# Two state space loops: every fourth product moves from VectorE to GpSimd, and the step sums from GpSimd to TensorE

## The chip, the cores and the metric

The kernel runs on one NeuronCore of one Trainium2 chip. Its engines work side by side, each on its own queue: TensorE (PE in the profile, its weight loads PEld), VectorE (DVE), ScalarE (ACT), GpSimd (POOL), and SyncE (SP), which here issues the DMA transfers. They wait for each other through semaphores. The metric is the time of one launch on the device in microseconds; lower is better.

## The reference, cut to what matters

A network of four layers with sixteen sub-blocks, all in float32, on x of 4 x 512 x 128. Two sub-blocks, L2b and L3b, are state space blocks (Mamba style), and only these are touched:

```python
x_dbl = u @ x_proj_w                     # u: 256 channels, from a convolution
dtr, Bc, Cc = x_dbl[..., :64], x_dbl[..., 64:80], x_dbl[..., 80:]
delta = softplus(dtr @ dt_proj_w + dt_proj_b)
A = -exp(A_log)                          # 256 channels x 16 states
def step(h, inp):
    d_t, b_t, c_t, u_t = inp
    dA = exp(d_t[:, :, None] * A)
    h = dA * h + (d_t * u_t)[:, :, None] * b_t[:, None, :]
    return h, einsum('bdn,bn->bd', h, c_t)
y = (ys + u * D) * silu(z)
out = y @ out_proj_w
```

For each of 4 batch rows there are 256 x 16 recurrences over 512 steps. Per recurrence: a decay (exp of step times A), a gain (step times u, times B), the scan, and a product with C that is summed over the 16 states.

## The kernel before, in words

The method `mamba` runs one such block. Its work is cut into units: a unit is 128 partitions x 2 x 512 steps, sixteen units make a batch row, 64 make the block. Two sub-blocks call it, so there are 128 units. The loop `for n in range(16 * B + 10)` issues, for each n, pieces of work for several units at once:

- `fetch(n + 5)`: SP copies the steps (`dl`, written to a DRAM tile before) back into one of six `da` tiles, spread over the partitions.
- `product(n + 1)` (line 2371): VectorE multiplies the gain by B (`br`), in place in PSUM.
- `scan(n)` (line 2376): VectorE's `tensor_tensor_scan` reads `da` from SBUF and the gain from PSUM and writes `hc` in SBUF. Line 2381: GpSimd multiplies `hc` by C (`cr`), in place. (For the last unit VectorE does it, line 2379.)
- `gain(n + 2)`: TensorE spreads `du` over the partitions, two matmuls into one of three `ps_du` buffers of two banks.
- `decay(n + 3)` (line 2357): ScalarE makes exp(A x step) in `da`, two activations.
- `read(m)`: every second n TensorE sums `hc` of two units, five and four behind, into `ps_y`.

Between these stand the pieces of `prepare(b)`, which makes the next batch row's inputs while the present one's units run: convolution halves (`c0a` to `c1b`), `u`, the projections `xd`, `br`, `cr`, the steps before softplus (`dt0`, `dt1`), `exps` and `logs` on ScalarE, the gates `z0`, `z1`, `sz`. Softplus is max(v,0) + ln(1 + exp(-|v|)), with a correction for the rounding of 1 + e. The sums that this takes (`s00` to `s13`, line 2274) are GpSimd operations of 128x512: three a half for the steps, and a fourth for `du` = steps x u. After the third the half is written to DRAM (line 2278).

The order on each engine is written out by hand: `keep` holds an instruction in program order on its engine, and the lists `order`, `usual` and `first` give each piece the n after whose unit work it is issued (`first` for batch row 1, whose preparation runs beside row 0's units; `usual` for rows 2 and 3). An engine's queue is in order, so a piece that waits holds back what is issued behind it.

PSUM is full: six banks for `ps_du`, one for `ps_y`, and one (tag "mm", the function `bank`) that all the preparing matmuls share in turn, each result being copied out by ScalarE before the next can begin.

I call the units 0 to 15 of a block group 0, and so on to group 3. In groups 0, 1 and 2 the next row is prepared; in group 3 nothing is.

Of the kernel before, what the change touches and what calls it, by code (L numbers as in the profile page):

```python
# [11 lines left out]
F32 = mybir.dt.float32  # L12
AF = mybir.ActivationFunctionType
ALU = mybir.AluOpType
# [4 lines left out]
P = 128  # L19
B, S, D = 4, 512, 128  # L20
# [254 lines left out]
class Net:  # L275
# [1895 lines left out]
    def mamba(self, g):  # L2171
# [5 lines left out]
        nc, tc = self.nc, self.tc  # L2177
        LAG, SPREAD, AHEAD, FETCH = 4, 2, 3, 5
        with ExitStack() as es:
            sp = es.enter_context(tc.tile_pool(name=g + "_s", bufs=1))  # L2180
            rp = es.enter_context(tc.tile_pool(name=g + "_r", bufs=2))
            pp = es.enter_context(tc.tile_pool(name=g + "_p", bufs=1, space=PSUM))
            dp = es.enter_context(tc.tile_pool(name=g + "_d", bufs=2, space=DRAM))
            keep = tc.keep_in_program_order
            m0 = self.m
            w, am, wc, dram = m0["w"], m0["am"], m0["wc"], m0["dram"]
            spread, gather, skip, ones = (m0[n] for n in ("spread", "gather", "skip", "ones"))
# [5 lines left out]
            def bank(name):  # L2193
                return pp.tile([P, S], F32, tag="mm", name=name)
# [3 lines left out]
            def prepare(b, **when):  # L2198

                u, sz, dl, du, br, cr = sets[b % 2]  # L2200
                xb = b * S
                t = {}
# [5 lines left out]
                def act(*a, **k):  # L2208
                    keep(nc.scalar.activation(*a, **k))
# [33 lines left out]
                    keep(nc.scalar.copy(out, ps[:n]))  # L2243

                def xd():
                    t["xd"] = rp.tile([64, S], F32, name="xd", bufs=1)
                    project(t["xd"], 0, 64)

                def step(c):
# [12 lines left out]

                def logs():
                    act(ln, w1, AF.Ln)
                    act(w1, w1, AF.Identity, bias=ones[:, 1:2])

                def sums(c, k):
                    o, x, y, op = (
                        (w1, w1, t["e"], ALU.subtract),
                        (ln, ln, w1, ALU.subtract),  # L2270
                        (dl, dl, ln, ALU.add),
                        (du, dl, u, ALU.mult),
                    )[k]
                    keep(nc.gpsimd.tensor_tensor(o[:, c], x[:, c], y[:, c], op))
                    if k == 2:
                        if c == 0:
                            dram[b] = dp.tile([P, 2, S], F32, name="dram")
                        nc.sync.dma_start(dram[b][:, c], dl[:, c])

                for name, n in when.items():  # L2280
                    f = {
                        "c0a": (conv, 0, False),
                        "c0b": (conv, 0, True),
                        "c1a": (conv, 1, False),
                        "c1b": (conv, 1, True),
                        "u": (lambda: act(u, t["raw"], AF.Silu),),
                        "xd": (xd,),
                        "dt0": (step, 0),
                        "dt1": (step, 1),
                        "br": (project, br, 64, P),  # L2290
                        "cr": (project, cr, 192, P),
                        "exps": (exps,),
                        "logs": (logs,),
                        "z0": (gate, 0),
                        "z1": (gate, 1),
                        "sz": (lambda: act(sz, t["z"], AF.Silu),),
                        **{f"s{c}{k}": (sums, c, k) for c in range(2) for k in range(4)},
                    }[name]
                    pieces.append((n, f))


            order = (
                "c0a", "c0b", "c1a", "c1b", "u", "xd", "dt0", "dt1", "br", "exps", "logs", "s00",
                "s01", "z0", "s02", "s10", "z1", "s11", "cr", "s12", "s03", "sz", "s13",
            )
            usual = (
                -6, -5, -4, -3, -2, -1, 0, 1, 2, 3, 4, 5,
                6, 6, 7, 8, 8, 9, 9, 10, 11, 11, 12,
            )
            for b in range(2, B):  # L2310
                at = {p: 16 * (b - 1) + n for p, n in zip(order, usual)}
                if b < B - 1:
                    at["sz"] += 3.5
                prepare(b, **at)
            first = (
                0, 0, 2, 2, 3, 4, 5, 6, 7, 7, 8, 8,
                9, 9, 9, 10, 9.5, 10, 8, 11, 11, 14.5, 12,
            )
            prepare(1, **dict(zip(order, first)))
            for n, f, *a in self.late:  # L2320
                pieces.append((n, (f, *a, bank)))
# [3 lines left out]
            dx, hc, yp, y, po = {}, {}, {}, {}, {}  # L2325
# [36 lines left out]
            def gain(n):  # L2362
                b, c, i, h = place(n)
                dx[n] = pp.tile([P, 2, S], F32, tag="du", name="ps_du", bufs=3)
                for t in range(2):
                    r = slice(64 * t, 64 * t + 64)
                    self.mm(dx[n][:, t], spread[r, 4 * h + i], sets[b % 2][3][r, c], pin=True)

            def product(n):
                br = sets[n // 16 % 2][4].unsqueeze(1).to_broadcast([P, 2, S])  # L2370
                keep(nc.vector.tensor_tensor(dx[n], dx[n], br, ALU.mult))  # L2371

            def scan(n):
                hc[n] = rp.tile([P, 2, S], F32, name="hc", bufs=7)
                h, a, x = (t.rearrange("p t s -> p (t s)") for t in (hc[n], da[n], dx[n]))
                keep(nc.vector.tensor_tensor_scan(h, a, x, 0.0, ALU.mult, ALU.add))  # L2376
                cr = sets[n // 16 % 2][5].unsqueeze(1).to_broadcast([P, 2, S])
                if n == 16 * B - 1:
                    keep(nc.vector.tensor_tensor(hc[n], hc[n], cr, ALU.mult))
                else:  # L2380
                    keep(nc.gpsimd.tensor_tensor(hc[n], hc[n], cr, ALU.mult))  # L2381
# [51 lines left out]
            for n in range(16 * B + 10):  # L2433
                if n + FETCH < 16 * B:
                    fetch(n + FETCH)
                if n + 1 < 16 * B:
                    product(n + 1)
                if n < 16 * B:
                    scan(n)
                if n + 2 < 16 * B:  # L2440
                    gain(n + 2)
                if n + AHEAD < 16 * B:
                    decay(n + AHEAD)
                while pieces and pieces[0][0] < n + 1:
                    f, *a = pieces.pop(0)[1]
                    f(*a)
                m = n - 1 - LAG
                if n % 2 == 1 and 0 <= m < 16 * B:
                    read(m)
                    if m % 8 == 6:  # L2450
                        last = m == 16 * B - 2
                        plan.at(n if last else n + 1, gated, m // 16, m // 8 % 2)
                        if m % 16 == 14:
                            plan.at(n if last else n + 4, output, m // 16)
                            plan.at(
                                n if last else n + 5,
                                lambda b: self.add_to_x(b, po[b], keep),
                                m // 16,
                            )
                plan.run(n)  # L2460
# [473 lines left out]
```

## Time and profile before

| what | value |
|---|---|
| runs shown | 2402.07 us median of 3 (2400.7 to 2405.41) |
| profiled execution | 2390.77 us, its span 2389.1 us |
| busy in the span | PE 2134.9, DVE 1703.8, ACT 1275.2, POOL 609.9 us |
| loop of L2b, first to last scan | 1577 to 1807 us |
| loop of L3b, first to last scan | 2110 to 2345 us |
| DMA in the loops | about 150 to 160 GB/s, half of the engines' time |

A line of the list of groups reads: source line, engine, operation, output<-inputs by name, shapes, count | busy us in all, mean ns of one | idle time of that engine just before, and who ended it. A line of a timeline reads: start, duration, engine, line, operation, and in brackets the idle time before it and its releaser. A float32 matmul appears as two MATMUL records. Matmuls overlap in their ends, so the distance from start to start tells more than a duration. The line number of a matmul is that of the helper, 346, so matmuls are told apart by their output's name.

### The profile page before, as it was taken

To read this page: it belongs to the slowest core of one execution; us is meant where nothing else is said; L and a number is where in the kernel's file an instruction comes from. 1 tells how busy PE (TensorE), PEld (TensorE's weight loads), DVE (VectorE), ACT (ScalarE), POOL (GpSimd) and SP (SyncE) were. 2 spreads that over 40 slices of the span, in tenths; PEclk is the share of its full clock that TensorE was granted. 3 is DMA by queue.
4 is the path that set the end of the run, shared out by engine and by line. 5 is a ranking of instruction groups with operands and counts; after the bars stand their busy time and mean duration, and the time that the engine had idled before them with its cause. 6 is when DMAs were issued, how large, how long until landed. Compare 5 with 4: busy or idle time off the path is not lost. (4 is left out here: it accounts for less than half of the span.)

```text
span 2389.1 us, 33451 instructions
## 1 busy us (share of the span) xinstructions
PE 2134.9 (89%) x12151; PEld 1004.9 (42%) x12151; DVE 1703.8 (71%) x3209; ACT 1275.2 (53%) x2539; POOL 609.9 (26%) x441
## 2 busy tenths in 40 slices
PE   7999999999899998999876889988969998878868
PEld 2343334643233333667434446542214666422213
DVE  6666666479998775556465664678997657688995
ACT  4555555169856655343442454666644445476643
POOL 1100010010000001022153410038872015148871
PEclk9999999999799998999876989999989999998989
DMA  3000000500000000600200016344552620044550
GB/s 145 1 1 1 1 1 19 126 1 1 2 2 2 1 2 1 144 1 2 109 0 1 1 32 102 71 120 144 156 154 43 113 41 2 1 132 138 158 154 18
DMA packets 68884, 127.84 MB, mean 54 GB/s; under 512 B 9328, under 2 KB 29296, under 8 KB 68080
## 3 DMA queue, kind: packets, MB, share of 16 engines
q1 hardware_dynamic: 68720, 125.71, 20.5%
q8 instruction: 96, 1.57, 0.3%
q14 instruction: 68, 0.56, 0.1%
HBM read 119.91 MB, written 5.64 MB: 53 GB/s over the span
## 5 line engine op out<-in xcount | busy, mean ns | idle before, releaser
L2381 POOL TENSOR_TENSOR hc<-hc,cr 128x1024 f32<-128x1024 f32 x126 | 297.2, 2359 | 113.9 <-DVE hc L2376 108.2
L2376 DVE TENSOR_TENSOR_SCAN hc<-da,ps_du 128x1024 f32<-128x1024 f32 x128 | 291.2, 2277 | 0.0
L346 PE MATMUL ps_s<-k,q 32*128 32x512 f32 (+3 forms) x1088 | 252.3, 601 | 8.6 <-DVE mx L853 4.7
L540 ACT ACTIVATE e<-ps_s,mx 128x512 f32<-128x512 f32 x256 | 172.6, 686 | 139.4 <-DVE mx L535 132.8
L346 PE MATMUL ps_du<-du,spread 64*128 64x512 f32 x512 | 161.6, 704 | 64.2 <-DVE hc L2376 63.9
L2357 ACT ACTIVATE da<-da,am 128x512 f32<-128x512 f32 x248 | 165.6, 715 | 62.5 <-DMA da<-dram 55.6
L346 PE MATMUL ps<-xT,w_L2f 128*128 128x512 f32 (+1 forms) x416 | 190.6, 605 | 0.2 <-DVE t L1948 0.2
L939 DVE TENSOR_REDUCE nm<-ps_s 128x1 f32<-128x512 f32 x256 | 162.5, 684 | 36.5 <-PE ps_s L346 24.2
L1025 ACT ACTIVATE e<-ps_st 128x512 f32<-128x512 f32 x256 | 138.3, 595 | 89.3 <-PE ps_s L346 61.5
L535 DVE TENSOR_REDUCE mx<-ps_s 128x2 f32<-128x1024 f32 x128 | 151.0, 1219 | 43.8 <-PE ps_s L346 43.6
L2371 DVE TENSOR_TENSOR ps_du<-ps_du,br 128x1024 f32<-128x1024 f32 x128 | 155.1, 1212 | 26.4 <-PE ps_du L346 26.4
L864 ACT ACTIVATE e<-e,mx 128x512 f32<-128x512 f32 (+3 forms) x256 | 140.1, 549 | 15.8 <-DVE mx L853 15.5
L346 PE MATMUL ps_st<-q,k 32*128 32x512 f32 x512 | 143.9, 646 | 0.0
L346 PE MATMUL ps_s<-q,k 64*128 64x512 f32 x512 | 129.1, 618 | 2.2 <-ACT e L540 1.7
L346 PE MATMUL ps_c<-e,vz 128*64 128x512 f32 x512 | 123.5, 604 | 0.8 <-POOL vz L551 0.8
L1948 DVE SCALAR_TENSOR_TENSOR t<-ps,w_L2f,t 128x512 f32<-128x512 f32 (+1 forms) x104 | 77.3, 747 | 61.8 <-PE ps L346 37.9
L661 DVE TENSOR_TENSOR hc<-hc,wt 128x1024 f32<-128x1024 f32 x80 | 93.6, 1171 | 36.5 <-DMA wt<-dram 17.5
L346 PEld LDWEIGHTS ps_du<-du,spread 64*128 64x128 f32 x512 | 45.3, 201 | 171.8 <-issue 126.4
L853 DVE CUSTOM_DVE_ANT_0 e<-ps_s,tri 128x512 f32<-128x512 f32 (+3 forms) x256 | 109.1, 484 | 11.7 <-PE ps_s L346 11.6
L346 PEld LDWEIGHTS ps_s<-k,q 32*128 32x128 f32 x1088 | 87.1, 194 | 71.8 <-issue 28.5
L551 POOL TENSOR_TENSOR vz<-v,z 128x512 f32<-128x512 f32 x32 | 33.3, 1042 | 322.0 <-DVE z L549 293.0
L346 PEld LDWEIGHTS ps<-xT,w_L2f 128*128 128x128 f32 (+1 forms) x416 | 74.8, 188 | 95.7 <-issue 78.7
(501 smaller groups left out, 4127.9 us busy)
## 6 DMA issues: line engine op xcount, KB each, us to landing
da<-dram SPq DMA_DIRECT2D x124, 256.0 KB
da<-dram SPq DMA_DIRECT2D x124, 255.5 KB
wt<-dram SPq DMA_DIRECT2D x144, 128.0 KB
wt<-dram SPq DMA_DIRECT2D x32, 256.0 KB
dram<-dl SPq DMA_DIRECT2D x16, 256.0 KB
wt<-dram SPq DMA_DIRECT2D x16, 224.0 KB
wt<-dram SPq DMA_DIRECT2D x16, 192.0 KB
wt<-dram SPq DMA_DIRECT2D x16, 160.0 KB
```

What stands on the lines that cost most here:

```text
L346: i = self.nc.tensor.matmul(out, lhsT, rhs, start=start, stop=stop)
L535: nc.vector.tensor_reduce(mx, sc, AX.X, ALU.max, negate=True)
L540: nc.scalar.activation(es[n][:, hh], sc[:, hh], AF.Exp, bias=mx[:, hh : hh + 1], accum_out=z[m][:, j, hh : hh + 1],)
L661: nc.vector.tensor_tensor(h, h, wt[b, k][:, r:e], ALU.mult)
L853: red = nc.vector.tensor_tensor_reduce(e[:, i, :w], sc[i][:, :w], tri[:, S - w :], -1.0, BIG, ALU.add, ALU.min, mx[:, i : i + 1],)
L864: nc.scalar.activation(e[:, i, :w], e[:, i, :w], AF.Exp, bias=mx[:, i : i + 1], scale=-1.0, accum_out=z[:, i : i + 1],)
L939: nc.vector.tensor_reduce(nm[:, j, i, 9:10], sc, AX.X, ALU.max, negate=True)
L1025: keep(nc.scalar.activation(es_[n][:, i], sc, AF.Exp))
L2357: nc.scalar.activation(da[n][:, t, t:], src[:, t:], AF.Exp, scale=am[:, at : at + 1])
L2371: keep(nc.vector.tensor_tensor(dx[n], dx[n], br, ALU.mult))
L2376: keep(nc.vector.tensor_tensor_scan(h, a, x, 0.0, ALU.mult, ALU.add))
L2381: keep(nc.gpsimd.tensor_tensor(hc[n], hc[n], cr, ALU.mult))
```

## The change

Three things, all in `mamba`:

1. For every fourth unit (n % 4 == 2, "shared") `product` is no longer a VectorE operation in PSUM. ScalarE copies the gain from PSUM to the unit's `hc` tile, GpSimd multiplies it there by B, the scan reads `da` and this `hc` (both in SBUF) and writes over it, and GpSimd then multiplies by C as before. `gain(n + 2)` and the shared product are issued before `scan(n)`. There are eight `hc` buffers in place of seven.
2. The three GpSimd sums of the steps go. `logs` now makes 1 - (1 + e) with the sign turned, and `total(c)` adds the four terms with four matmuls against the identity into the shared bank; ScalarE copies the sum to `dl`. `du` stays on GpSimd.
3. The pieces get new places: in `first` the gates move from 9 and 9.5 to 11.5 and 13.5 and the sums `dl0`, `dl1` stand at 9.3 and 9.6; in `usual` `z0` 5, `dl0` 6, `dl1` 8, `du0` 8, `z1` 9, `du1` 10, `cr` 10, `sz` 11. The `xd` tile is now the first 64 partitions of the not yet written `du`.

```diff
                 def xd():
-                    t["xd"] = rp.tile([64, S], F32, name="xd", bufs=1)
+                    t["xd"] = du[:64, 0]
                     project(t["xd"], 0, 64)
...
                 def logs():
                     act(ln, w1, AF.Ln)
-                    act(w1, w1, AF.Identity, bias=ones[:, 1:2])
-
-                def sums(c, k):
-                    o, x, y, op = (
-                        (w1, w1, t["e"], ALU.subtract),
-                        (ln, ln, w1, ALU.subtract),
-                        (dl, dl, ln, ALU.add),
-                        (du, dl, u, ALU.mult),
-                    )[k]
-                    keep(nc.gpsimd.tensor_tensor(o[:, c], x[:, c], y[:, c], op))
-                    if k == 2:
-                        if c == 0:
-                            dram[b] = dp.tile([P, 2, S], F32, name="dram")
-                        nc.sync.dma_start(dram[b][:, c], dl[:, c])
+                    act(w1, w1, AF.Identity, bias=ones[:, 0:1], scale=-1.0)
+
+                def total(c):
+                    ps = bank("ps_dl")
+                    terms = (w1, t["e"], ln, dl)
+                    for n, x in enumerate(terms):
+                        self.mm(ps, self.ident, x[:, c], start=n == 0, stop=n == 3, pin=True)
+                    keep(nc.scalar.copy(dl[:, c], ps))
+                    if c == 0:
+                        dram[b] = dp.tile([P, 2, S], F32, name="dram")
+                    nc.sync.dma_start(dram[b][:, c], dl[:, c])
+
+                def inputs(c):
+                    keep(nc.gpsimd.tensor_tensor(du[:, c], dl[:, c], u[:, c], ALU.mult))
...
             order = (
-                "c0a", "c0b", "c1a", "c1b", "u", "xd", "dt0", "dt1", "br", "exps", "logs", "s00",
-                "s01", "z0", "s02", "s10", "z1", "s11", "cr", "s12", "s03", "sz", "s13",
+                "c0a", "c0b", "c1a", "c1b", "u", "xd", "dt0", "dt1", "br", "exps", "logs",
+                "z0", "dl0", "dl1", "du0", "z1", "du1", "cr", "sz",
             )
-            usual = (
-                -6, -5, -4, -3, -2, -1, 0, 1, 2, 3, 4, 5,
-                6, 6, 7, 8, 8, 9, 9, 10, 11, 11, 12,
-            )
+            usual = (-6, -5, -4, -3, -2, -1, 0, 1, 2, 3, 4, 5, 6, 8, 8, 9, 10, 10, 11)
...
-            first = (
-                0, 0, 2, 2, 3, 4, 5, 6, 7, 7, 8, 8,
-                9, 9, 9, 10, 9.5, 10, 8, 11, 11, 14.5, 12,
-            )
+            first = (0, 0, 2, 2, 3, 4, 5, 6, 7, 7, 8, 11.5, 9.3, 9.6, 10, 13.5, 11, 8.5, 14.5)
...
+            def shared(n):
+                return n % 4 == 2
+
             def product(n):
                 br = sets[n // 16 % 2][4].unsqueeze(1).to_broadcast([P, 2, S])
-                keep(nc.vector.tensor_tensor(dx[n], dx[n], br, ALU.mult))
+                if shared(n):
+                    hc[n] = rp.tile([P, 2, S], F32, name="hc", bufs=8)
+                    keep(nc.scalar.copy(hc[n], dx[n]))
+                    keep(nc.gpsimd.tensor_tensor(hc[n], hc[n], br, ALU.mult))
+                    dx[n] = hc[n]
+                else:
+                    keep(nc.vector.tensor_tensor(dx[n], dx[n], br, ALU.mult))
 
             def scan(n):
-                hc[n] = rp.tile([P, 2, S], F32, name="hc", bufs=7)
+                if not shared(n):
+                    hc[n] = rp.tile([P, 2, S], F32, name="hc", bufs=8)
...
-                if n + 1 < 16 * B:
+                if n + 1 < 16 * B and not shared(n + 1):
                     product(n + 1)
+                if n + 2 < 16 * B:
+                    gain(n + 2)
+                    if shared(n + 2):
+                        product(n + 2)
                 if n < 16 * B:
                     scan(n)
-                if n + 2 < 16 * B:
-                    gain(n + 2)
```

More of the change, by code (lines that the diff above doesn't have):

```diff
@@ L2296, in prepare @@
                         "sz": (lambda: act(sz, t["z"], AF.Silu),),
-                        **{f"s{c}{k}": (sums, c, k) for c in range(2) for k in range(4)},
+                        **{f"dl{c}": (total, c) for c in range(2)},
+                        **{f"du{c}": (inputs, c) for c in range(2)},
                     }[name]
```

## The prediction

> **What bounds the kernel now.** I read the page's list of costly groups first, then the busy times over each stretch of sixteen units, then the timelines of single engines. The change touches only the two state space loops, L2b (1577 to 1807 us) and L3b (2107 to 2345 us).
>
> ```profile
> L2381 POOL TENSOR_TENSOR hc<-hc,cr 128x1024 f32<-128x1024 f32 x126 | 297.2, 2359 | 113.9 <-DVE hc L2376 108.2
> L2376 DVE TENSOR_TENSOR_SCAN hc<-da,ps_du 128x1024 f32<-128x1024 f32 x128 | 291.2, 2277 | 0.0
> ...
> L2371 DVE TENSOR_TENSOR ps_du<-ps_du,br 128x1024 f32<-128x1024 f32 x128 | 155.1, 1212 | 26.4 <-PE ps_du L346 26.4
> ```
>
> The scan never waits; GpSimd (POOL) waits for it. The stretches of L2b (columns: stretch, length, busy us of PE, PEld, DVE, ACT, POOL, then clock and DMA):
>
> ```profile
> 1577.35:1639.29 61.94, 54.47 (x178) 16.70 (x177) 53.97 (x34) 44.79 (x63) 45.96 (x24) 0.94 0.52 151
> 1639.29:1696.24 56.95, 50.09 (x186) 15.03 (x187) 56.37 (x45) 37.95 (x54) 47.30 (x25) 0.94 0.54 157
> 1696.24:1752.74 56.50, 44.55 (x168) 12.38 (x166) 56.33 (x44) 38.64 (x55) 47.27 (x25) 0.88 0.55 158
> 1752.74:1804.80 52.06, 35.25 (x146) 9.34 (x144) 51.89 (x42) 17.99 (x25) 34.48 (x15) 0.84 0.40 112
> ```
>
> VectorE fills groups 1 to 3 (the last line lacks one unit). In group 0 it doesn't: one stall of 6.81 us in L2b and of 8.01 us in L3b. One unit on VectorE, from its timeline:
>
> ```profile
> 1699.55 2.28 DVE L2376 TENSOR_TENSOR_SCAN hc<-da,ps_du 128x1024 f32<-128x1024 f32 x1
> 1701.74 1.21 DVE L2371 TENSOR_TENSOR ps_du<-ps_du,br 128x1024 f32<-128x1024 f32 x1
> 1702.86 2.28 DVE L2376 TENSOR_TENSOR_SCAN hc<-da,ps_du 128x1024 f32<-128x1024 f32 x1
> ```
>
> From start to start a scan takes 2.19 and a product 1.12, so a unit takes 3.31 and four units 13.2. Sixteen are 52.9, plus two gatings (0.58 each) and an addition with statistics (2.3): 56.4.
>
> The stall of group 0, on TensorE:
>
> ```profile
> 1608.01 1.13 PE L346 MATMUL ps_du<-du,spread 64*128 64x512 f32 x4
> 1612.17 2.08 PE L346 MATMUL ps_z<-xT,w_L2b 128*128 128x512 f32 x2 [3.03 <-ACT cr L2243]
> 1615.29 2.07 PE L346 MATMUL ps_z<-xT,w_L2b 128*128 128x512 f32 x2 [1.04 <-ACT z L2230]
> 1617.29 1.72 PE L346 MATMUL ps_y<-hc,gather 128*32 128x512 f32 x8
> 1618.94 1.13 PE L346 MATMUL ps_du<-du,spread 64*128 64x512 f32 x4
> ```
>
> Two z products wait in program order for the one "mm" bank, and the next unit's gain stands behind them. VectorE waits until 1620.12.
>
> **VectorE's saving.** 32 products (every fourth unit, 16 a loop) leave: 32 x 1.12 = 36 us at most, and four units would need 12.1.
>
> **What POOL gets.** 36 step sums of 1.27 leave (46 us); 32 products of 2.36 come (75 us). Back to back one takes 2.32 (1719.35 to 1721.66), so five per four units are 11.6, under VectorE's 12.1. By busy time alone POOL just fits.
>
> **The scan's second input.** Before, a scan reads da from SBUF and ps_du from PSUM; after, every fourth reads da and hc, both in SBUF. Where this trace runs two-SBUF-input VectorE work beside a two-input POOL operation, they take turns. VectorE and POOL while L2b's first batch is prepared:
>
> ```profile
> 1518.63 0.69 DVE L2120 TENSOR_TENSOR xn<-xn,sz 128x512 f32<-128x512 f32 x1
> 1519.35 1.65 DVE L2120 TENSOR_TENSOR dl<-dl,xn 128x512 f32<-128x512 f32 x1
> 1521.03 1.65 DVE L2120 TENSOR_TENSOR du<-dl,u 128x512 f32<-128x512 f32 x1
> ```
>
> ```profile
> 1518.37 2.08 POOL L2120 TENSOR_TENSOR xn<-xn,sz 128x512 f32<-128x512 f32 x1 [25.41 <-ACT xn L2103]
> 1520.53 1.60 POOL L2120 TENSOR_TENSOR dl<-dl,xn 128x512 f32<-128x512 f32 x1
> 1522.21 1.60 POOL L2120 TENSOR_TENSOR du<-dl,u 128x512 f32<-128x512 f32 x1
> ```
>
> In L3b the same operations don't overlap and take 0.69 and 1.26. Here VectorE's second ends 0.55 after POOL's first (1520.45), and POOL's second 1.13 after that (1522.13): one stops while the other runs. A scan of two SBUF inputs beside a POOL operation of one input is slowed too, less:
>
> ```profile
> L1579 DVE TENSOR_TENSOR_SCAN ema<-w_L1b,ema x4: 1224/1386/1704, 1189.2 to 1246.7; 128x512 f32<-128x512 f32 x4
> ```
>
> So a shared scan's wait is bounded by 0.5 us (1.70 against 1.22) and by a whole POOL operation, 2.3; POOL's by nothing and a whole scan, 2.2. I take turn-taking, because the L2120 rows have POOL's operation with both its inputs.
>
> [...]
>
> **Four units with turns.** Let n be a multiple of 4 and T the end of scan n-1, which frees the ps_du for unit n+2. Its gain takes 1.1, ScalarE's copy about 1.06 (two 128x512 copies start 0.48 apart; a 128x1024 activation takes 1.04 to 1.15: bounds 0.96 and 1.2), with hand-offs T+3.0. POOL multiplies to T+5.3, then does hc of n to T+7.6. VectorE (1.1+2.2+2.2+1.1) reaches scan n+2 at T+6.6, waits until 7.6, ends at 9.8. POOL, stopped until then, does three more hc to 16.7, while scan n+3 ends at 13.1: POOL is 3.6 late. The next four then start their product at T+3.6; the scan waits from 6.6 to 8.2 and ends at 10.4; scan n+3 ends at 13.7 and POOL at 17.3, again 3.6 late. The steady period is 13.7 = 5 x 2.3 + 2.2, against 13.2 now.
>
> **Groups 1 to 3.** Group 3 (no preparation): 54.8, plus the 2.3 addition of which 0.6 returns (POOL catches up to 2.65 late, the first period above), plus 0.3 of gating: 56.8 against 56.4, **+0.4**. Groups 1 and 2 have two du products more on POOL (2.5): at least 57.3. TensorE gets 48 matmuls, 12 sums of four: two full 128x512 matmuls take 1.91 from start to start (ps_d at 1606.10, next at 1608.01), so 3.8 a sum, 7.7 a batch, 46 in all. Added up at full speed group 1 holds some 47 of TensorE now (16 gains of 1.06, 8 readings of 1.0, four convolution halves of 1.9, five projections of 1 to 2, gating and output 4) and 54.7 after. Its second half is the tight one: dl1, z1 and cr now stand beside the next batch's convolution, 29.8 us plus about 1.7 of waits for the single bank, against 29.9 of POOL. I take group 1 +2.2 and group 2 +1.3: **+3.5**; bounds -4.5 (the whole saving, 4 x 1.12) and +9 (sums not hidden, 7.7, plus 1.3).
>
> **Group 0.** dl0 and dl1 take z0's and z1's place behind cr's copy. 3.8 + 0.6 + 3.8 = 8.2 us, or 10 if TensorE is slow after its wait (the two z took 2.08 there against 1.1 elsewhere), against 5.1 now (1612.17 to 1617.29). So the gain behind them comes 3 to 5 later. z0 and z1 move to iterations 11 and 13, where TensorE is busy 19.4 of 20 us (1620 to 1640): another 2. Three copies come before that point on ScalarE (3.2 us), whose idle time there, 6.4, holds most: +1. I take **+6**; bounds 0 (hidden in stalls) and +11. Both writes of the steps to DRAM now stand in SP's queue ahead of the fetch for unit 15 and are released by dl1's copy, at about 1623; that unit's scan starts at 1635.98 now, so 13 us cover it. ScalarE's dl copies, 12 x 0.59, go beside scans; in group 0 they are the 0.6 above. Behind a shared unit's copy on ScalarE, which waits for scan n-1, stands the decay of unit n+3: three scans cover it. The xd tile inside du and the eighth hc buffer add no instruction; du's first half was last read over seven units before (its gains are over at unit 8 of the batch), so I cost them at nothing.
>
> **End of a loop.** POOL, late, has two hc after scan 62 (4.6): 1.0 later than now, 2.2 if VectorE's last product takes turns too. I take **+1.6**.
>
> **Sum.** 2 x (6 + 3.5 + 0.4 + 1.6) = **+23 us**. The profiled execution took 2390.77 us (span 2389.1) and would take 2414; the three runs' median is 2402.07, 0.5% above it, and it is to this that I add: **2425 us**.
>
> **Rivals.**
> - **No turns** (the other side): a scan of da and hc keeps its 2.28. For it: no row shows a long scan of two SBUF inputs beside two-input POOL work, and L1579 loses only 0.5. Against: the L2120 rows. Then group 1 is TensorE's (-1.2), group 2 -3.5, group 3 -4.5, no late end; group 0 +6. 2 x -3.2 = -6: 2396 us. It decides from a shared scan's mean below about 2.9, for the 0.7 that it may lose per four is then under the 1.12 saved. Chance 0.2.
> - **TensorE becomes the bound** in groups 0 to 2: sums wait for the bank in order, gains late, ScalarE's copies late, POOL idle in front of them. For it: 95% use needed and one bank. Against: gains run two units ahead. Group 0 +10, groups 1 and 2 +5 each, with 0.4 and 1.6: 2 x 22 = +44: 2446 us. Chance 0.2.
> - **Group 0 costs nothing**: its sums replace POOL's slow chain (xn at 1611.7 to du at 1632). 2 x 5.5 = +11: 2413 us. Against: VectorE's stall ended on a gain, not on POOL. Chance 0.15.
>
> The forecast has 0.45. Within 0.2% (4.8 us, about what a measurement can tell from no change) fall the edges of the first and last rival. Faster 0.18, same 0.1, slower 0.72. The range runs from just under the first rival, 2393, to just over the second, 2450; the forecast's own is 2412 to 2438.
>
> **What would show it.** Right: the 32 shared scans average 3 to 4.5 us and the others stay at 2.28; about 32 POOL operations last over 3 us; group 3 is 55.5 to 58 long; the stall of group 0 grows to 9 to 13 us; products number 96. Wrong: shared scans at 2.28, groups 3 at 52 us, or a group 0 shorter than 62 and 68 us.

## The result and the profile after

The changed kernel takes 2438.36 us (median of four runs, 2434.4 to 2443.25), the kernel before, run beside it, 2401.39 (2396.76 to 2405.41): a ratio of 1.0156, interval 1.0133 to 1.0178. It is slower by 37 us. The profiled execution took 2439.79 us, its span 2438.1.

The costly groups of the changed kernel (columns as before: line, engine, operation, names, shapes, count | busy us, mean ns | idle us before and its releasers):

```profile
L2387 POOL TENSOR_TENSOR hc<-hc,cr 128x1024 f32<-128x1024 f32 x126 | 353.3, 2829 | 24.6 <-DVE hc L2382 24.6
...
L2382 DVE TENSOR_TENSOR_SCAN hc<-da,ps_du 128x1024 f32<-128x1024 f32 x96 | 216.8, 2269 | 0.0
...
L2376 DVE TENSOR_TENSOR ps_du<-ps_du,br 128x1024 f32<-128x1024 f32 x96 | 116.3, 1212 | 59.5 <-PE ps_du L346 59.3
L2382 DVE TENSOR_TENSOR_SCAN hc<-da,hc 128x1024 f32<-128x1024 f32 x32 | 112.1, 3502 | 0.0
...
L2373 POOL TENSOR_TENSOR hc<-hc,br 128x1024 f32<-128x1024 f32 x32 | 75.5, 2360 | 51.5 <-ACT hc L2372 33.0 <-DVE ln_st L374 18.4
```

VectorE's products fell from 155.1 to 116.3 us, as meant. But the 32 scans that read `da` and `hc` last 3.50 us in place of 2.28, GpSimd's product with C grew from 297.2 to 353.3 us at the same count, and VectorE's waits for a gain grew from 26.4 to 59.3 us.

The same tile's instructions one by one (columns: count, then min/median/max ns, then first and last start):

```profile
L2387 POOL TENSOR_TENSOR hc<-hc,cr x126: 2333/2362/4365, 1586.7 to 2391.7; 128x1024 f32<-128x1024 f32 x126
L2382 DVE TENSOR_TENSOR_SCAN hc<-da,hc x32: 2847/3454/4392, 1588.2 to 2386.5; 128x1024 f32<-128x1024 f32 x32
L2385 DVE TENSOR_TENSOR hc<-hc,cr x2: 3300/3302/3305, 1832.0 to 2391.8; 128x1024 f32<-128x1024 f32 x2
```

No shared scan is as short as an unshared one (2.85 us or more against 2.28 or less). Of GpSimd's 126 products 30 last 4.32 to 4.37 us and all others 2.39 or less, so each of the 30 stood still for about 1.98 us. The last unit's product on VectorE (two SBUF inputs as well) took 1.353 us before and takes 3.30 now.

The four groups of L2b by engine (columns: stretch, length, busy us of PE, PEld, DVE, ACT, POOL, then granted clock and DMA):

```profile
1581.40:1653.50 72.10, 61.72 (x194) 20.11 (x193) 55.37 (x30) 49.91 (x69) 55.16 (x22) 0.95 0.44 131
1653.50:1716.40 62.90, 55.50 (x202) 17.97 (x202) 56.59 (x40) 43.00 (x60) 56.20 (x22) 0.97 0.49 142
1716.40:1777.60 61.20, 46.79 (x182) 14.67 (x182) 57.46 (x40) 40.88 (x57) 56.88 (x23) 0.93 0.50 146
1777.60:1829.70 52.10, 34.78 (x144) 9.71 (x140) 51.84 (x38) 21.90 (x32) 47.94 (x20) 0.78 0.37 111
```

VectorE fills only group 3 now. Its own busy time didn't fall in groups 1 to 3 (56.59, 57.46 and 51.84 against 56.37, 56.33 and 51.89): the longer scans eat the products that left, and the stalls come on top. So the longer time shows mostly as stalls: the waits for a gain grew by 32.9 us, the eight groups of the next table by 40.2 together.

Times from first scan to first scan of the next group (of group 3: to its last scan), L2b / L3b, in this and in the runs of the next section; the last column is both loops together against the kernel before:

| kernel | group 0 | group 1 | group 2 | group 3 | loops |
|---|---|---|---|---|---|
| before | 61.9 / 67.8 | 57.0 / 56.5 | 56.5 / 56.4 | 52.0 / 52.0 | |
| after | 72.1 / 75.9 | 62.9 / 62.9 | 61.2 / 61.2 | 52.1 / 52.1 | +40.2 |
| gain read from PSUM | 72.3 / 76.4 | 61.0 / 62.7 | 56.6 / 61.4 | 47.7 / 48.3 | +26.2 |
| SBUF copy of the product | 64.6 / 69.5 | 60.9 / 60.5 | 60.5 / 60.8 | 57.4 / 57.4 | +31.4 |
| sums only | 69.7 / 75.3 | 61.0 / 61.9 | 57.7 / 57.6 | 52.0 / 52.0 | +27.2 |
| sharing only | 65.0 / 69.1 | 64.1 / 64.1 | 64.1 / 64.1 | 53.3 / 53.3 | +37.0 |
| decay in PSUM | 76.1 / 79.7 | 69.5 / 69.3 | 64.6 / 67.2 | 47.8 / 48.5 | +62.5 |
| sums spread | 72.4 / 79.6 | 57.9 / 57.9 | 57.0 / 57.2 | 52.1 / 52.2 | +26.1 |
| sums later | 66.6 / 73.0 | 58.6 / 58.6 | 57.1 / 57.0 | 52.2 / 52.0 | +15.1 |
| some shares | 62.2 / 68.0 | 60.6 / 62.0 | 61.3 / 61.0 | 50.6 / 50.5 | +16.1 |
| last group only | 62.1 / 67.8 | 57.0 / 56.6 | 56.5 / 56.4 | 47.6 / 47.5 | -8.6 |
| some shares without unit 2 | 62.1 / 67.8 | 56.9 / 55.9 | 55.5 / 56.6 | 48.9 / 48.2 | -8.1 |

Behind the last scan the loop's end (to the gating of y) took 5.7 and 5.7 us before and takes 7.6 and 7.6 now. That makes +44.1 us in the two loops, out of 49.0 between the two profiled spans; the rest arose outside them (4.1 before L2b begins), where nothing is changed. The medians differ by 37: the profiled execution of the kernel before (2390.77) is 10.6 us under its median, that of the changed kernel 1.4 over. The stretch ahead of L2b, the same in all kernels, takes 1577.4 to 1590.1 us in the profiles used here, so differences of some us outside the loops mean nothing. The table is read for where, the ratios for how much.

Two places show the price. First, group 3, where nothing is prepared. VectorE's timeline (columns: start, us, engine, line, operation), cut to the shared scans and what follows each:

```profile
1783.29 3.52 DVE L2382 TENSOR_TENSOR_SCAN hc<-da,hc 128x1024 f32<-128x1024 f32 x1
1786.73 1.20 DVE L2376 TENSOR_TENSOR ps_du<-ps_du,br 128x1024 f32<-128x1024 f32 x1
...
1797.24 3.12 DVE L2382 TENSOR_TENSOR_SCAN hc<-da,hc 128x1024 f32<-128x1024 f32 x1
```

and GpSimd beside it:

```profile
1779.98 2.36 POOL L2373 TENSOR_TENSOR hc<-hc,br 128x1024 f32<-128x1024 f32 x1
1782.30 11.26 POOL L2387 TENSOR_TENSOR hc<-hc,cr 128x1024 f32<-128x1024 f32 x4
1793.52 2.35 POOL L2373 TENSOR_TENSOR hc<-hc,br 128x1024 f32<-128x1024 f32 x1
1795.84 11.29 POOL L2387 TENSOR_TENSOR hc<-hc,cr 128x1024 f32<-128x1024 f32 x4
1807.08 2.38 POOL L2373 TENSOR_TENSOR hc<-hc,br 128x1024 f32<-128x1024 f32 x1
```

GpSimd has no gap: four units take it 13.54 and 13.56 us, five products of 2.32 and one stop of 1.96. It is the bound here, and the scan waits for it in the form of a longer duration, not of idle time.

Second, the stall of group 0 on TensorE (columns as above; in brackets the idle time before and its releaser):

```profile
1612.97 1.13 PE L346 MATMUL ps_du<-du,spread 64*128 64x512 f32 x4
1618.04 2.08 PE L346 MATMUL ps_dl<-xn,ident 128*128 128x512 f32 x2 [3.94 <-ACT cr L2243]
1619.91 1.91 PE L346 MATMUL ps_dl<-e,ident 128*128 128x512 f32 x2
...
1624.74 1.12 PE L346 MATMUL ps_dl<-xn,ident 128*128 128x512 f32 x2 [0.68 <-ACT dl L2273]
...
1628.37 1.06 PE L346 MATMUL ps_y<-hc,gather 128*32 128x512 f32 x8
1629.37 1.13 PE L346 MATMUL ps_du<-du,spread 64*128 64x512 f32 x4
```

and what VectorE sees of it:

```profile
1630.54 1.23 DVE L2376 TENSOR_TENSOR ps_du<-ps_du,br 128x1024 f32<-128x1024 f32 x1 [10.92 <-PE ps_du L346]
```

From one gain to the next are 16.4 us; before they were 10.9 (1608.01 to 1618.94).

### The profile page after: what moved, and what is told of

It is laid out like the page before. It is cut to its first block, busy times and chain, and to the rows that moved or that the text cites. A ratio compares the mean times of both kernels' runs of the same rounds, so it can differ in the third digit from the quotient of the medians.

```text
span 2438.1 us, 33447 instructions
## 1 busy us (share of the span) xinstructions
PE 2169.8 (89%) x12247; PEld 1023.7 (42%) x12247; DVE 1712.7 (70%) x3177; ACT 1307.5 (54%) x2583; POOL 697.1 (29%) x437
## 3 DMA queue, kind: packets, MB, share of 16 engines
q8 instruction: 97, 1.59, 0.3%
## 5 line engine op out<-in xcount | busy, mean ns | idle before, releaser
L2387 POOL TENSOR_TENSOR hc<-hc,cr 128x1024 f32<-128x1024 f32 x126 | 353.3, 2829 | 24.6 <-DVE hc L2382 24.6
L2382 DVE TENSOR_TENSOR_SCAN hc<-da,ps_du 128x1024 f32<-128x1024 f32 x96 | 216.8, 2269 | 0.0
L346 PE MATMUL ps_du<-du,spread 64*128 64x512 f32 x512 | 156.6, 691 | 59.5 <-DVE hc L2382 41.8
L939 DVE TENSOR_REDUCE nm<-ps_s 128x1 f32<-128x512 f32 x256 | 162.4, 683 | 36.6 <-PE ps_s L346 26.4
L2376 DVE TENSOR_TENSOR ps_du<-ps_du,br 128x1024 f32<-128x1024 f32 x96 | 116.3, 1212 | 59.5 <-PE ps_du L346 59.3
L853 DVE CUSTOM_DVE_ANT_0 e<-ps_s,tri 128x512 f32<-128x512 f32 (+3 forms) x256 | 109.2, 484 | 12.3 <-PE ps_s L346 12.1
L2382 DVE TENSOR_TENSOR_SCAN hc<-da,hc 128x1024 f32<-128x1024 f32 x32 | 112.1, 3502 | 0.0
```

Source lines behind the costliest of these rows:

```text
L346: i = self.nc.tensor.matmul(out, lhsT, rhs, start=start, stop=stop)
L853: red = nc.vector.tensor_tensor_reduce(e[:, i, :w], sc[i][:, :w], tri[:, S - w :], -1.0, BIG, ALU.add, ALU.min, mx[:, i : i + 1],)
L939: nc.vector.tensor_reduce(nm[:, j, i, 9:10], sc, AX.X, ALU.max, negate=True)
```

## The experiments

My theory: a scan with two SBUF inputs and GpSimd take turns, which eats VectorE's saving; sums on TensorE make gains late in groups 0 and 1. The rivals: it is all the sums, or all GpSimd's load and the hand-over to it.

**The gain read from PSUM.** The changed kernel, where the shared scan takes its gain from PSUM as the others do. GpSimd's product is made and not used, so this kernel leaves out B in every fourth unit.

```diff
                     keep(nc.scalar.copy(hc[n], dx[n]))
                     keep(nc.gpsimd.tensor_tensor(hc[n], hc[n], br, ALU.mult))
-                    dx[n] = hc[n]
```

> The changed kernel, but a shared unit's scan reads the gain from PSUM, as the others do. ScalarE's copy and GpSimd's product still run and are thrown away, so B is left out of every fourth unit. Only the second SBUF input is gone. Theory (the engines take turns): the 32 shared scans fall from 3.50 to 2.28 us, GpSimd's products with C from 2.83 to about 2.36, sixteen units of group 3 come to 47 to 49 us in place of 52, and 22 to 37 us of the 37 lost return: 2401 to 2416. Rival (TensorE in its queue is the bound, turns are only visible): scans fall too, but groups 1 and 2 stay at 61 to 63 us and less than 12 us return: 2426 or more.

Measured: 2418.49 us, ratio 1.0077 (1.0056 to 1.0099). The groups of scans and of products with C in this kernel:

```profile
L2386 POOL TENSOR_TENSOR hc<-hc,cr 128x1024 f32<-128x1024 f32 x126 | 294.8, 2363 | 37.8 <-DVE hc L2381 37.5
L2381 DVE TENSOR_TENSOR_SCAN hc<-da,ps_du 128x1024 f32<-128x1024 f32 x128 | 289.9, 2274 | 0.0
```

All durations are back to those of before, with the copy and GpSimd's 32 products still issued, and group 3 gives 4.3 and 3.7 us. So the second SBUF input costs the changed kernel 1.0156 - 1.0077, some 19 us, and neither the copy nor GpSimd's load makes these; but 18 us stay, all in groups 0 to 2. (The scan here doesn't wait for GpSimd's product either; the next run and the decay in PSUM show that the input, and not this hand-over, is what counts.) The time lies between the two expectations, and the table shows why: group 3 gives back what was expected, but group 0 nothing. There VectorE's busy time in L2b falls from 55.4 to 49.9 us and its idle time grows from 16.7 to 22.4, for the gains come no earlier. So in group 0, where VectorE waits for TensorE anyway, turns cost next to nothing (72.1 and 75.9 us with them, 72.3 and 76.4 without).

**An SBUF copy of the product, and its control.** The kernel before; in every fourth unit ScalarE copies the finished product to `hc` and the scan reads the copy. The control makes the copy, and the scan reads PSUM.

```diff
                 keep(nc.vector.tensor_tensor(dx[n], dx[n], br, ALU.mult))
+                if n % 4 == 2:
+                    hc[n] = rp.tile([P, 2, S], F32, name="hc", bufs=8)
+                    keep(nc.scalar.copy(hc[n], dx[n]))
+                    dx[n] = hc[n]        # not in the control
```

> The kernel before, with one thing added: every fourth unit's product, still made by VectorE in PSUM, is copied by ScalarE to SBUF, and the scan reads the copy. VectorE and GpSimd do exactly the work of before. Theory (turns): GpSimd starts the product with C of the unit before 0.14 us after that unit's scan and needs 2.36, VectorE is ready for the next scan after 1.1 (its product), so each of the 32 scans waits about 1.4 us: scans of 3.6 to 3.7, +40 us, 2441, with 22 to 60 as bounds. Rival (no turns for a scan): the scans stay at 2.28 and the time within 5 us of before.

> The control of the run that copies the product: the same ScalarE copies of every fourth product, but the scan reads PSUM. Both theories: ScalarE has 11 us free in every 56, so 2401 to 2406. If it is slower than that, part of the cost of the run with the copies is ScalarE's and not the second SBUF input's.

Measured: 2429.54 us, 1.0134 (1.0105 to 1.0164) with the copy read; a ratio of 1.0023 (1.0008 to 1.0038) with the copy only made. The tile's rows with the copy read:

```profile
L2386 POOL TENSOR_TENSOR hc<-hc,cr x126: 2335/2356/4366, 1581.8 to 2377.0; 128x1024 f32<-128x1024 f32 x126
...
L2381 DVE TENSOR_TENSOR_SCAN hc<-da,hc x32: 2274/3618/4378, 1586.2 to 2373.3; 128x1024 f32<-128x1024 f32 x32
```

The second SBUF input alone, the only difference between the two, is worth 0.0111, about 27 us: 32 scans, 0.8 us each. Here mostly VectorE pays (median 3.62 us) and GpSimd less (median 2.36 us, the longest product 4.37, for it has idle time of its own). So turn-taking is shown both by adding it to the kernel before and by taking it from the changed one.

**The sums only.** The changed kernel without sharing.

```diff
             def shared(n):
-                return n % 4 == 2
+                return False
```

> The changed kernel with no unit shared: all products on VectorE in PSUM; the step sums on TensorE and the new places of the pieces stay. Theory (TensorE's sums cost mainly in group 0): group 0 is 6 to 8 us longer than before in each loop, groups 1 and 2 by 0 to 2 each, group 3 not at all: +12 to +25, 2413 to 2426. Rival (group 0 grows only through turns and copies): within 5 us of before.

Measured: 2422.96 us, 1.0095 (1.0073 to 1.0117). VectorE's stall in group 0 is the changed kernel's:

```profile
1628.84 1.23 DVE L2376 TENSOR_TENSOR ps_du<-ps_du,br 128x1024 f32<-128x1024 f32 x1 [10.74 <-PE ps_du L346]
```

Group 0 pays 7.7 and 7.6 us, as expected; group 1 pays 4.0 and 5.4, where 0 to 2 were expected; group 2 pays 1.2, group 3 nothing. That makes 27 us in the loops of the profile, 23 by the ratio, for the sums and their order.

**Sharing only.** The changed kernel with the sums, their order and places as before (36 sums on GpSimd again).

> The sharing alone: every fourth product on GpSimd as in the changed kernel, the sums of the steps still on GpSimd at their old places. If the two parts simply add, this is 2 x (0 in group 3 + 2 at the end + a few in the others): 1.005 to 1.009 (about 2417). If GpSimd becomes the bound in groups 0 to 2, as its sum says (16 products with C and 4 with B at 2.32 are 46.4, eight sums of 1.27 are 10.2, four turns of 2.2 are 8.8: 65 against 56.5), groups 1 and 2 take about 64 each and group 0 some 3 more: +40 us, 1.014 to 1.02 (about 2438), and then the move of the sums to TensorE pays for itself.

Measured: 2440.12 us, 1.0163 (1.0142 to 1.0184): as slow as the whole change. Groups 1 and 2 of L2b by engine (columns as above, POOL the fifth busy time):

```profile
1653.00:1717.10 64.10, 52.41 (x184) 15.54 (x184) 59.39 (x41) 42.37 (x57) 64.10 (x29) 0.87 0.50 139
1717.10:1781.20 64.10, 42.68 (x166) 12.83 (x164) 59.34 (x41) 39.69 (x53) 64.10 (x29) 0.85 0.51 140
```

GpSimd is busy every microsecond of both. So the parts don't add: sharing alone costs 39 us, the sums alone 23, both 37. With the sums on GpSimd, sharing makes GpSimd the bound; moving them takes that away and puts nearly as much on TensorE's queue.

**The decay in PSUM.** The changed kernel; for a shared unit ScalarE writes the decay into the `ps_du` tile that it has just copied out, so the scan has one SBUF input and the result stays whole. Of the diff only the end is shown; `decay` also takes the tile to write to, passes over shared units at its old place, and copies one column (0.16 us).

```diff
                     keep(nc.scalar.copy(hc[n], dx[n]))
                     keep(nc.gpsimd.tensor_tensor(hc[n], hc[n], br, ALU.mult))
-                    dx[n] = hc[n]
+                    decay(n, dx[n])
+                    dx[n], da[n] = hc[n], dx[n]
```

> The changed kernel, whole in what it computes, with one thing turned round: for a shared unit ScalarE writes the decay (its Exp) into the freed ps_du tile in PSUM instead of da, so that the scan reads the decay from PSUM and the gain from hc in SBUF. GpSimd's product and ScalarE's copy stay. If two SBUF inputs are what makes a shared scan and GpSimd take turns: all 128 scans at 2.28 us, GpSimd's products at 2.36, group 3 at 47.7 to 48.5, and a ratio as with the gain read from PSUM, 1.005 to 1.012 (about 2418). If instead GpSimd's own load (five products a four) or the hand-over ScalarE to GpSimd to VectorE is what costs, the scan waits just as long for its gain: group 3 stays at 52 and the time at 1.013 to 1.017 (about 2435).

Measured: 2457.45 us, 1.0244 (1.0222 to 1.0266). A miss, and the most useful one. The turns are gone, as the tile's rows show:

```profile
L2394 POOL TENSOR_TENSOR hc<-hc,cr x126: 2335/2356/2402, 1584.0 to 2408.7; 128x1024 f32<-128x1024 f32 x126
...
L2389 DVE TENSOR_TENSOR_SCAN hc<-ps_du,hc x32: 2274/2278/2281, 1586.4 to 2405.6; 128x1024 f32<-128x1024 f32 x32
```

and group 3 falls to 47.8 and 48.5 as expected. But groups 0 to 2 each take 3 to 7 us more than in the changed kernel. The unit's decay has moved on ScalarE from its old place to behind its copy, ahead of the pieces that prepare the next row; TensorE waits for those in its queue, and gains wait behind, as the list of waits suggests and the run without unit 2 below tests for one unit. The list of TensorE's waits in L2b (columns: what waited, for what, us in total, times, longest):

```profile
PE ps_dt L346 <- ACT e L2209: 7.9, 2, 4.1
...
PE ps_dl L346 <- ACT cr L2243: 5.6, 1, 5.6
```

In the changed kernel these are 2.5 and 3.9 us. The buffer is also held until the scan, where the changed kernel frees it at the copy; how much of the loss that makes I did not separate.

The scans of this run (the shared ones with the decay in PSUM, median 2278 ns) and of the first (all with the gain in PSUM, mean 2274) are as short as before the change (mean 2277), and no product of GpSimd's with C is over 2402 ns in this run: which of the scan's two inputs is in PSUM doesn't matter here.

**The sums spread.** The sums only, at other places: `cr` before the exponentials, `dl1` an iteration after `dl0`, and both gates of rows 2 and 3 before the logarithms.

```diff
-usual = (-6, -5, -4, -3, -2, -1, 0, 1, 2, 3, 4, 5, 6, 8, 8, 9, 10, 10, 11)
+usual = (-5.4, -5, -4, -3, -2, -1, 0, 1, 2, 3, 4, 2.5, 6, 8, 8, 3.5, 10, 9, 11)
-first = (0, 0, 2, 2, 3, 4, 5, 6, 7, 7, 8, 11.5, 9.3, 9.6, 10, 13.5, 11, 8.5, 14.5)
+first = (0, 0, 2, 2, 3, 4, 5, 6, 7, 7.6, 8, 11.5, 9.3, 10.5, 10, 13.5, 11.5, 7.5, 14.5)
```

> The sums on TensorE alone, no sharing, with the same TensorE work at other places: cr's projection before the exponentials, so that its copy doesn't stand behind the logarithms on ScalarE, dl1 one unit after dl0 with a gain between them, both gates of rows 2 and 3 before the logarithms. If the order (the one bank, ScalarE's copies behind the logarithms, gains behind two sums) makes the cost of the sums: group 0 falls from 69.7 and 75.3 to 64 to 66 and 70 to 71, group 1 from 61.0 to 57 to 58, and the time to 1.002 to 1.005 (about 2408). If the amount of TensorE work makes it: groups 0 and 1 stay within 2 us of 69.7, 75.3 and 61.0, and the time at 1.008 to 1.011 (about 2421).

Measured: 2421.22 us, 1.0093 (1.0072 to 1.0113). The time is that of the second expectation, but the groups follow neither: group 1 falls from 61.0 and 61.9 to 57.9, so there it was mostly the order and not the amount of work. Group 0 rises by 2.7 and 4.2, which uses that up. With `cr` out of the way dl0 waits for the logarithms themselves:

```profile
1627.06 2.07 PE L346 MATMUL ps_dl<-xn,ident 128*128 128x512 f32 x2 [4.67 <-ACT xn L2209]
```

**The sums later.** As above, but in group 0 `cr` back at 8.5 and `dl0`, `dl1` at 10.1 and 11.1, behind two more gains.

```diff
-usual = (-6, -5, -4, -3, -2, -1, 0, 1, 2, 3, 4, 5, 6, 8, 8, 9, 10, 10, 11)
+usual = (-4.8, -4, -3.5, -3, -2, -1, 0, 1, 2, 3, 4, 2.5, 6, 8, 8, 3.5, 10, 9, 11)
-first = (0, 0, 2, 2, 3, 4, 5, 6, 7, 7, 8, 11.5, 9.3, 9.6, 10, 13.5, 11, 8.5, 14.5)
+first = (0, 0, 2, 2, 3, 4, 5, 6, 7, 7, 8, 12.2, 10.1, 11.1, 11.5, 13.5, 12.5, 8.5, 14.5)
```

> The sums on TensorE alone, no sharing, as in the run with the sums spread, but in group 0 cr back at 8.5 and dl0 and dl1 later, at 10.1 and 11.1, so that two more gains stand before them and one between them; the convolution of row 2 begins an iteration later. If group 0's stall comes from TensorE standing in front of the logarithms' chain on ScalarE with the gains queued behind: no stall over 5 us, group 0 at 63 to 67 in L2b (69.7 with the sums as changed, 72.4 spread) and 69 to 72 in L3b (75.3, 79.6), groups 1 and 2 near 58 and 57, and 1.003 to 1.006. If 15 us of matmuls more than TensorE has room for makes it (two sums at 3.8 and their waits in a group that needs TensorE nearly all the time): the stall only moves, group 0 stays at 69 to 72 and 75 to 79, and the time at 1.008 to 1.01.

Measured: 2414.83 us, 1.0066 (1.0041 to 1.0091), between the two expectations. No wait of VectorE in the loops is over 4.2 us any more and group 0 takes 66.6 and 73.0. Against the sums as changed that is 3.0 and 2.3 us of order; 4.7 and 5.3 stay, with three waits of 3.3 to 4.1 us in place of one stall. These I put down to the added matmuls, for TensorE has no gap over 0.78 us from dl0 to the end of the group in L2b; no run shows it.

**Some shares.** The kernel before, its sums in place, sharing with the decay in PSUM in units 2 and 14 of groups 0 to 2 and in units 2, 6, 10 of group 3.

The rest of the edit is that of sharing only and of the decay in PSUM.

```diff
+            def shared(n):
+                return n % 16 in (2, 14) if n < 48 else n % 4 == 2 and n < 60
```

> The kernel before, sums and their order as they were, with sharing only where GpSimd has room and without the second SBUF input (decay in PSUM as in the run above): units 2 and 14 of groups 0 to 2 and units 2, 6 and 10 of group 3. If VectorE bounds the groups and turns were what ate its saving: 1.12 us for each shared unit that VectorE doesn't wait in, so 3.3 in group 3, 2.2 in groups 1 and 2, 0 to 1 in group 0, 8 to 9 a loop, -16 to -18 us (ratio 0.993, about 2383). If the product's way over ScalarE and GpSimd costs as much as it saves, or GpSimd falls behind, the time stays within 0.2% of before or rises.

Measured: 2414.61 us, 1.0049 (1.0031 to 1.0066). A miss again: group 3 gives 1.4 and 1.5 us where 3.3 were expected, and groups 1 and 2 take 3.7 to 5.5 more than before. Their unit 2 on ScalarE:

```profile
1711.43 1.01 ACT L2382 COPY hc<-ps_du 128x1024 f32<-128x1024 f32 x1 [1.54 <-PE ps_du L346]
1712.48 0.16 ACT L2354 COPY ps_du<-da 128x1 f32<-128x1 f32 x1
1712.66 1.28 ACT L2363 ACT_TABLE_LOAD   x1
1713.95 1.41 ACT L2363 ACTIVATE ps_du<-da,am 128x512 f32<-128x512 f32 x2
1715.30 1.32 ACT L2363 ACTIVATE da<-da,am 128x512 f32<-128x512 f32 x2
1716.53 0.67 ACT L2209 ACTIVATE dl<-ps_dt,w_L2b 128x512 f32<-128x512 f32 x1
```

and what TensorE and VectorE make of it:

```profile
1717.82 2.07 PE L346 MATMUL ps_dt<-du,w_L2b 64*128 64x512 f32 x2 [4.09 <-ACT e L2209]
...
1721.68 2.08 PE L346 MATMUL ps_du<-du,spread 64*128 64x512 f32 x4
1723.81 1.23 DVE L2387 TENSOR_TENSOR ps_du<-ps_du,br 128x1024 f32<-128x1024 f32 x1 [5.87 <-PE ps_du L346]
```

Ahead of dt0's activations (the last line on ScalarE) stand a wait for the unit's gain, the copy, a table load and the decay. The table load isn't new: before, this unit's decay came an iteration earlier and the load with it (1694.11). dt1 waits 4.09 us for the bank and runs slowly behind the wait, as does the gain behind it (2.08 us against 1.13), and VectorE waits 5.87 us for a gain, to be spared a product of 1.12.

**The last group only, and some shares without unit 2.** The same edit with the sharing in other units.

```diff
-                return n % 16 in (2, 14) if n < 48 else n % 4 == 2 and n < 60
+                return n % 4 == 2 and n >= 48                        # last group only
+                return n % 16 == 14 if n < 48 else n % 4 == 2        # without unit 2
```

> The kernel before with sharing in group 3 alone (its units 2, 6, 10 and 14), the decay of these units in PSUM so that no scan has two SBUF inputs; sums, order and the other groups as before. If group 3, where nothing is prepared, is bound by VectorE, and ScalarE, GpSimd and TensorE have the room there: groups 0 to 2 as before (62, 57, 56.5 and 68, 56.5, 56.5), group 3 at 47.8 to 48.5 as with the decay in PSUM in all groups, the end of the loop unchanged: -7 to -8 us, ratio 0.997. If the PSUM buffer, held from the gain to the scan, makes TensorE's gains late here too (as in the run with some shares, whose group 3 took 50.6): group 3 at 50 to 51, -3 us, ratio 0.9985 to 1.0.

> Sharing with the decay in PSUM in unit 14 of groups 0 to 2 and in the four units of group 3; against the run with some shares unit 2 of groups 0 to 2 is left out. If there the stall of 5.87 us in groups 1 and 2 came from unit 2's copy and decay on ScalarE standing ahead of dt0's two activations, for which TensorE's dt1 and the gains behind it wait: no such stall, groups 1 and 2 at 55.5 to 57 (61 there), group 3 at 47.6 to 48.5, ratio 0.994 to 0.9965. If sharing costs as much wherever a batch row is prepared: groups 1 and 2 at 58 to 61 and 0.998 to 1.002.

Measured: the last group only takes 2388.96 us, ratio 0.9952 (0.9933 to 0.9970); without unit 2 it is 2390.05 us, 0.9964 (0.9950 to 0.9978). Both beat the kernel before. Leaving out unit 2 took the stall of 5.87 away (groups 1 and 2 at 55.5 to 56.9), so the sharing of unit 2 made it; how it divides between copy, table load and decay isn't shown. Unit 14 gives 1.0 us in one group of L2b and 0.6 in one of L3b, but group 3 behind them is 1.4 and 0.7 longer than with the last group alone, with a wait for a gain of 1.25 us in it in L2b and of 0.40 in L3b: in sum it gains nothing, and why isn't shown. With the last group alone, groups 0 to 2 stay within 0.2 us of before, so the gain's new place ahead of the scan and the eighth buffer cost nothing by themselves. VectorE in group 3 of the kernel with the last group only:

```profile
1758.90 1.23 DVE L2387 TENSOR_TENSOR ps_du<-ps_du,br 128x1024 f32<-128x1024 f32 x1
1760.05 2.28 DVE L2393 TENSOR_TENSOR_SCAN hc<-ps_du,hc 128x1024 f32<-128x1024 f32 x1
...
1771.64 1.21 DVE L2387 TENSOR_TENSOR ps_du<-ps_du,br 128x1024 f32<-128x1024 f32 x1
1772.75 2.28 DVE L2393 TENSOR_TENSOR_SCAN hc<-ps_du,hc 128x1024 f32<-128x1024 f32 x1
```

Four units with one gating (0.58) take 12.70 us, so 12.1 without it, the forecast's number for no turns. Eight products left, 9.0 us at 1.12, and group 3 is shorter by 4.4 in L2b and 4.5 in L3b. The interval of the ratio, 7 to 16 us, holds this.

## Why the prediction was right or wrong

The direction and the range held: 2425 forecast, 2438 measured, 2393 to 2450 given. The size was short: 23 us against 37 by the medians and 44 in the profiled loops, and 2438 lies at the very edge of the forecast's own 2412 to 2438. The mechanism held in group 3, at the end of the loops and in the stall of group 0. In groups 1 and 2 it did not: there a rival's was at work, and that the time lies in the range owes something to that rival, whose 2446 set the upper end.

- **Turns** were right. Shared scans average 3.50 us (3 to 4.5 said, the unshared unchanged), 30 products of GpSimd are long (about 32 said), and the SBUF copy and the gain from PSUM show the cause from both sides. "No turns" falls with it: its point of decision was a mean of 2.9. Turns cancel VectorE's saving (its busy time in the groups is 0 to 1.4 us above that of before); without them about half of the loss, 18 of 37 us, would stay.
- **Four units with turns** were right in mechanism and size: 13.7 said, with GpSimd as the bound; 13.54 and 13.56 measured, since the stop is 1.96 and not 2.2. Group 3 costs +0.1 (+0.4 said). The end of a loop costs +2.0 and +1.9 (+1.6 said), the case in which VectorE's last product takes turns too (2.2 said; 3.30 us for 1.353). The lateness of 2.65 us named with group 3 comes out of none of the forecast's numbers; nothing else rests on it.
- **Group 0** was too low: +6 said, +10.2 and +8.2 measured, inside its bounds of 0 and +11. The stall itself was right (10.92 in L2b, 10.29 in L3b; 9 to 13 said, and a growth of 3 to 5, of which 4.1 and 2.3 came). Its working was right in the slow case: the two sums with the copy between them take 10.3 us (1618.04 to 1628.37), where 8.2 was said, "or 10 if TensorE is slow". Short were "another 2" for z0 and z1 at their new places, for behind the stall VectorE waits 1.09, 1.17 and 1.74, against 0.78 before; and two things that the sum had at nothing, the turns of group 0's own shared scans (VectorE is busy 1.4 and 1.0 us longer) and waits for a gain before the stall (1.24 us behind the second scan of L2b; 4.92 in L3b, where 3.41 were before).
- **Groups 1 and 2** were the step that failed: "group 1 +2.2 and group 2 +1.3" with an upper bound of +9; measured +10.6 and +11.1. The forecast had GpSimd as the bound there (57.3 us); GpSimd is busy 56.20 of 62.90 us and VectorE waits for gains. I had added up TensorE's work and found room for it (the 29.8 and 29.9 us for the second half of group 1 can't be followed from the lines shown). The room was there, but TensorE can't use it in its order: in group 1 of L2b dl0 waits for the gate's copy, which ScalarE makes behind the shared unit's copy, the logarithms and two table loads, and then runs at part of its clock (0.58 granted from 1677.2 to 1681.3 us). On TensorE:

```profile
1672.10 1.13 PE L346 MATMUL ps_du<-du,spread 64*128 64x512 f32 x4
1676.03 1.13 PE L346 MATMUL ps_dl<-xn,ident 128*128 128x512 f32 x2 [2.80 <-ACT z L2230]
...
1681.35 1.13 PE L346 MATMUL ps_du<-du,spread 64*128 64x512 f32 x4
```

  9.3 us from gain to gain where VectorE needs one in 3.3; it ends in a stall of 3.25. Both bounds of these two groups were too narrow by their own terms: -4.5 has the four products of one group and +9 the sums of one batch row (7.7), where two groups have eight products and two rows. With the sums only there is no such wait at dl0; VectorE loses its 4.0 us there in three smaller ones (1.11, 2.01, 1.06) behind dl0, cr and the next row's convolution. In the order of the sums spread, group 1 pays 1.0 and 1.4 us in place of 4.0 and 5.4; the whole change in that order was not run. Group 2 is open in part: the sums alone cost it 1.2, the whole change 4.7 and 4.8, and without turns it took 56.6 in one loop and 61.4 in the other.
- **"TensorE becomes the bound"** had about the right numbers (+10, +5 and +5 for the groups, 2446 in all) and, as far as the runs go, the right mechanism for groups 0 to 2: sums wait in order, gains and ScalarE's copies come late. The sums alone bring 7.7, 4.7 and 1.2 in the mean of both loops, the rest comes with the sharing. TensorE isn't full (55.50 of 62.90 us in group 1 of L2b); its queue is blocked.
- **"Group 0 costs nothing"** is refuted by the sums only.
- The loops of the profiled executions differ by 44 us, the medians by 37. That gap of 7 is of the size of what executions differ in outside the loops; what makes it isn't shown.

## What to carry to other kernels

When work moves from VectorE to GpSimd, ask first where the inputs lie: here a scan that read two SBUF tiles took turns with GpSimd (3.50 us in place of 2.28 in the changed kernel), and one input kept in PSUM avoided it (2.27 and 2.28), which the SBUF copy and its control put at 0.8 us of each shared scan, where VectorE has no idle time to lose. Ask next what the helper's instruction stands in front of in its in-order queue: one copy and one decay on ScalarE, in the wrong iteration and with a table load between them, cost 5.9 us for a product of 1.1. The same sharing pays in the stretch that has no preparation (8.6 us in the two loops, a ratio of 0.9952), gains nothing at unit 14 and loses at unit 2, where a queue of small pieces runs beside it; so a uniform "every fourth unit" was the wrong shape. An added matmul is not priced by its duration alone: count the wait for its buffer and the slow clock after it (for dl0 in group 0 a wait of 3.94 us, then about 5 us at a granted 0.53).

## What was not expected of the hardware

- GpSimd's product with C has two durations in the changed kernel and nothing between: 2.33 to 2.39, or 4.32 to 4.37 us. Each of the 30 long ones ran beside a shared scan and stood still for about 1.98 us, less than the 2.28 of a scan that doesn't wait.
- TensorE's granted clock fell within the stall of group 0 and stayed low for the work behind it. Granted clock in the changed kernel before, in and after the stall of group 0 (columns: stretch, length, busy us of PE, PEld, DVE, ACT, POOL, then clock and DMA):

```profile
1605.00:1613.00 8.00, 7.50 (x28) 2.23 (x25) 8.00 (x5) 6.34 (x9) 6.74 (x4) 1.00 0.49 131
1618.00:1623.00 5.00, 4.96 (x6) 2.19 (x7) 1.63 (x1) 2.62 (x3) 5.00 (x2) 0.53 0.00 0
1624.00:1630.00 6.00, 5.33 (x21) 1.90 (x20) 0.00 (x0) 2.11 (x4) 1.35 (x2) 1.00 0.37 126
```

  The wait of 3.94 us is followed by about 5 us at 0.53, in which the pairs of matmuls take 2.08, 1.91 and 1.59 us in place of 1.02. The clock is 1.00 for the first 1.8 us of this wait (1614.1 to 1615.9) and 0.51 in the rest of it. After the wait of 2.80 us in group 1 the clock was still 1.00 at first (1676.0 to 1677.2) and the first pair took 1.13; the next ones took 1.53, 1.91 and 1.40, at a granted clock of 0.58 (1677.2 to 1681.3). So a slow clock followed the shorter wait too, after its end.
